# A two-layer graph attention kernel: a layer's last eight superchunks in the step with split sums, in a new order

## The chip, the cores and the metric

The kernel runs on one core of one Trainium2 chip, as one program. The metric is device time in microseconds (us) for one execution: median 4116.05 us of 3 runs of the kernel before (4113.4 to 4126.3).

## What is computed

There are 6250 nodes with 256 features and 200000 edges, sorted by destination. The reference is a pre-norm residual block around two graph attention layers (4 heads, then 1). Cut to what matters:

```python
h = relu(layernorm(x))
# one layer, called twice (heads h=4 f=64, then h=1 f=256):
te = relu(edge_attr @ We + be) * exp(x @ Wo + bo)[src]       # edge features
s2, d2, ea2 = add_self_loops(src, dst, te)                   # loop = mean of a node's edges
hx = (x @ Wg).reshape(n, h, f)
al = leaky_relu((hx*a_s).sum(-1)[src] + (hx*a_d).sum(-1)[dst] + ((ea2@Wge)*a_e).sum(-1), 0.2)
al = exp(al - segment_max(al, dst)[dst])
al = al / segment_sum(al, dst)[dst]
out = segment_sum(hx[src] * al, dst) + b
# layer 0: x = relu(out + x); layer 1: x = out + x; then + h, and + the input
```

## The kernel before, in words

**Tables.** A prologue writes a table T0 with one row per node (projected features, logit parts, norm factors). Layer 0 reads it and writes T1, the same kind of table, which layer 1 reads.

**Superchunks.** The edges are cut into 66 superchunks per layer (`NS`): 64 of 24 chunks of 128 edges, then one of 14 and one of 13. Both layers together make 132 steps k; s = k mod 66 is a step's number in its layer, `st` is its state, `pv` the step before it, `pr` the one before that, `nx` the next. Two edges of the work cross superchunks: a node whose edges are split over two of them is joined by a carried row.

**One superchunk, by engine.**

- GpSimd (POOL) fetches its source rows: `gather` (L881) issues one indirect DMA per chunk into `G`. There are three buffers, taken in turn (k mod 3), so the gather of step k+1 needs the sums of step k-2 to be done. In layer 1 it also needs T1.
- Edge features: `rphase1` (L965 on TensorE, L970 or L968 on ScalarE: two halves, product then relu, into `R`; one PSUM tile `y`, so the second half's product waits for the first half's relu), then `rphase2` (L979) and `adst` (L1038) into the PSUM tile `zad`, then `edge_rows` on VectorE (transpose L1052 or L1050, reduce L1055).
- Logits: `logits` (L1066 to L1081, VectorE; L1066 is the first instruction that needs the gathered rows), `ends` (transpose into `lf`, L1089, TensorE), `links` (L1099, L1101 on VectorE, then the transpose L1106 on TensorE), `maxima` (L1116 to L1143; its L1123 or L1120 needs L1106).
- Values: `scale` (L1174, VectorE, all rows times their weights), `carried` (L1156 to L1164, adds the carried row to chunk 0), `onehots` (L1009, VectorE, the matrix `S`).
- Sums: `sums` (L1185, TensorE): two instructions per chunk, `S` times `G`, into the PSUM tile `u`. `evict` (L1190, ScalarE) copies it to `U`, `carry` (L1196, L1198) forms the carried row.
- Nodes: `finish` (L1209 to L1274 in layer 0, L1214 to L1302 in layer 1; VectorE with three or one ScalarE operations), and in layer 0 `rows1` (L1280, L1282), `rows2` (L385), `rows3` (L389 on VectorE, L1292 on ScalarE, L1321 the write to T1 from SyncE).
- `spread` (L994, L995) once per pair of steps, `parts` (L1019 to L1024), `blocks` (L1031), and in layer 0 a few index instructions per step (`index_on`, L532 to L568).

**Order.** Everything is issued in the program's order, written out by hand; no scheduler moves instructions. Each engine runs its own in that order. There are four kinds of step:

- The plain step (loop body of `edges`): all sums of `pv` between the parts of `nx` and the links of `st`, and `finish` of the step two back.
- The step that enters (s + 1 = `tight`): plain, and then the first half of its own sums, one more `onehots` (for `nx`) and one more `finish` (for `pv`).
- `tight` (s >= `tight`): the first half of the sums of `st` is issued in its own step, right after `scale`; the rest follows in the next step, in two pieces, one before and one after the links' transpose (method `meet`). With `tight = NS - 4` these are s = 62, 63 and 64; s = 61 enters. The one of s = 64 has `final` set: there the nodes of s = 62 and s = 63 are finished and their T1 rows written, because the next layer's first gather (`src1`) needs T1 up to there. The rows of the last two superchunks are added to that gather by products (`added`, L849, L852).
- `last` (s = 65).

Of the kernel before, what the change touches and what calls it, by code (L numbers as in the profile page):

```python
# [32 lines left out]
C = 24  # L33
# [45 lines left out]
class Kernel:  # L79
# [311 lines left out]
    def indices(self, wp):  # L391
# [20 lines left out]
        self.base_f = base = cp.tile([P, NS], F32, name="base")  # L412
        V.tensor_copy(base, scf[:, 0, :])
        last, qbase, qlast = scf[:, 1, :], scf[:, 3:7, :], scf[:, 7:11, :]
        yield

# [41 lines left out]
        yield  # L458
        ll = wp.tile([P, NS], F32, name="ll", bufs=1)
        V.tensor_sub(ll, last, base)  # L460
        self.lsel = cp.tile([P, NS], F32, name="lsel")
        V.tensor_scalar(self.lsel, ll, self.iota_p, None, op0=OP.is_equal)
# [109 lines left out]
    def edges(self, ctx):  # L572
        nc = self.nc
        self.gp += [self.pool(f"gath{i}", 1, ctx) for i in range(1, 3)]
        self.sp = self.pool("onehot", 2, ctx)
        self.lp = self.pool("loads", 2, ctx)
        self.wp = self.pool("work", 2, ctx)
        self.np_ = self.pool("nodes", 2, ctx)
        self.xp = self.pool("index", 1, ctx)
        self.ps_y = self.pool("ps_y", 1, ctx, space=PSUM)  # L580
        self.ps_1 = self.pool("ps_1", 1, ctx, space=PSUM)
        self.ps_f = self.pool("ps_f", 1, ctx, space=PSUM)
        self.lf = self.ps_1.tile([P, 512], F32, name="lf")
        nc.vector.memset(self.lf[0:4, 0:1], -BIG)
        offs = np.concatenate([[0], np.cumsum(self.cs)]).tolist()
        steps = [dict(L=L, s=s, C=self.cs[s], o=offs[s], k=L.l * self.NS + s)
                 for L in self.L for s in range(self.NS)]
        self.state = {0: None, 1: None}
        self.early = self.cs[0] if self.NS > 1 else 0
        self.steps = steps  # L590
        self.nodes(steps[0])
        self.load_lb(0)
        self.load_ea(0)
        self.load_fl(0)
        self.gather(steps[0], self.CX)
        if self.NS % 2:
            self.load_lb(1)
        self.spread(steps[0])
        self.parts(steps[0])
        self.blocks(steps[0])  # L600
        drain(self.rphase1(steps[0]))
        self.load_ea(1)
        self.rphase2(steps[0])
        self.adst(steps[0])
        self.edge_rows(steps[0])

        pv = pf = pr = None

        tight = max(self.NS - 4, 1)
        self.ahead, self.rest = 1, None  # L610
        for k, st in enumerate(steps):
            nx = steps[k + 1] if k + 1 < len(steps) else None
            for q in steps[k + 1:k + 3]:
                if q["L"] is st["L"] and "tw" not in q:
                    self.nodes(q)
            self.load_lb(k + 2)
            left = self.groups[self.ahead][0] - 2 - k if self.ahead < len(self.groups) else 99
            if self.rest is None and left <= 2:
                gi = self.index_load(self.ahead, self.xp)
                self.rest = self.index_group(self.ahead, self.xp, gi)  # L620
            if st["s"] + 1 == self.NS:
                self.last(st, pv, nx)
                pv = pf = pr = None
                continue
            if st["s"] >= tight:
                self.tight(st, pv, pr, nx)
                self.index_on(left)
                pr, pv = pv, st
                continue
            self.gather(nx)  # L630
            drain(self.rphase1(nx))
            self.load_ea(k + 2)
            drain(self.logits(st))
            self.ends(st)
            self.spread(nx)
            self.parts(nx)
            if pv and "u" not in pv:
                self.sums(pv)
            self.links(st)
            self.load_fl(k + 1)  # L640
            self.blocks(nx)
            if k != self.NS:
                self.onehots(st)
            if pf:
                drain(self.finish(pf))
            if pv and "U" not in pv:
                self.evict(pv)
                self.carry(pv)
            if pf:
                self.rows1(pf)  # L650
            self.rphase2(nx)
            self.adst(nx)
            drain(self.maxima(st))
            if pf:
                self.rows2(pf)
            if k == self.NS:
                self.onehots(st)
            drain(self.scale(st))
            self.carried(st)
            enter = st["s"] + 1 == tight  # L660
            if enter:
                self.sums(st, 0, self.pieces(st)[0])
            elif st["s"] == 0:
                self.sums(st)
            if pf:
                self.rows3(pf)
            self.edge_rows(nx)
            if enter:
                self.onehots(nx)
                if pv:  # L670
                    drain(self.finish(pv))
                pr = pv
            elif st["s"] == 0:
                self.evict(st)
                self.carry(st)
            self.index_on(left)
            pf, pv = pv, st
            if k == 0 and self.early:
                self.redirect()
        self.flag()  # L680
# [9 lines left out]
    def pieces(self, st):  # L690

        c = st["C"]
        return (c + 1) // 2, c - c // 3

    def meet(self, st, pv, nx):

        p1, p2 = self.pieces(pv) if pv else (0, 0)
        drain(self.logits(st))
        self.ends(st)
        if nx:  # L700
            self.spread(nx)
            self.parts(nx)
        if pv:
            self.sums(pv, p1, p2)
        self.links(st)
        if pv:
            self.sums(pv, p2)
        self.load_fl(st["k"] + 1)

    def tight(self, st, pv, pr, nx):  # L710


        final = nx["s"] + 1 == self.NS
        self.gather(nx)
        self.meet(st, pv, nx)
        self.blocks(nx)
        if final:
            self.evict(pv)
            self.carry(pv)
            if pr:  # L720
                self.rows1(pr)
                self.rows2(pr)
                self.rows3(pr)
            drain(self.finish(pv))
            drain(self.maxima(st))
            self.rows1(pv)
            self.rows2(pv)
        else:
            drain(self.maxima(st))
            self.evict(pv)  # L730
            self.carry(pv)
            if pr:
                self.rows1(pr)
                self.rows2(pr)
        drain(self.rphase1(nx))
        self.load_ea(st["k"] + 2)
        self.rphase2(nx)
        self.adst(nx)
        if final:
            self.rows3(pv)  # L740
        drain(self.scale(st))
        self.carried(st)
        self.sums(st, 0, self.pieces(st)[0])
        if pr and not final:
            self.rows3(pr)
        self.edge_rows(nx)
        self.onehots(nx)
        if not final:
            drain(self.finish(pv))

    def last(self, st, pv, nx):
# [6 lines left out]
            nc.sync.dma_start(v[:, :early * P], self.srow.partition_broadcast(P))  # L758
        if not pv:
            self.onehots(st)  # L760
        self.meet(st, pv, None)
        if nx:
            nc.vector.tensor_scalar(self.src, self.src, 2.0, None, op0=OP.mult)
        drain(self.maxima(st))
# [687 lines left out]
def drain(g):  # L1452
    for _ in g:
        pass
# [93 lines left out]
```

## Time and profile before

| what | us |
|---|---|
| median of 3 runs | 4116.05 (4113.4 to 4126.3) |
| profiled execution, its own time | 4109.04 |
| span of its trace | 4107.1 |
| POOL busy | 2988.5 (73% of the span), 3158 instructions |
| VectorE (DVE) busy | 2872.1 (70%) |
| TensorE (PE) busy | 2807.1 (68%), granted clock 0.789 of full speed on average |
| ScalarE (ACT) busy | 545.5 (13%) |
| first gather of the stream / last gather's end | 89.62 / 4067.93 |
| layer 0: last gather's end; layer 1: first gather's start | 2058.5; 2097.34 |

The start of a step's `logits` is its first L1066 in the timeline. I call the time from the end of a step's gather to there its lag. At the end of both layers it reads as follows (all from the timelines of POOL and VectorE):

| step | gather | logits start | lag |
|---|---|---|---|
| 57 | 1802.2 to 1831.8 | 1840.6 | 8.8 |
| 58 | 1832.1 to 1862.2 | 1871.1 | 8.9 |
| 61 (enters) | 1923.1 to 1953.3 | 1959.9 | 6.7 |
| 62 | 1953.6 to 1983.5 | 1998.4 | 15.0 |
| 63 | 1983.8 to 2013.6 | 2029.9 | 16.3 |
| 64 (final) | 2013.9 to 2031.5 | 2061.7 | 30.2 |
| 65 (last) | 2042.5 to 2058.5 | 2096.2 | 37.7 |
| 127 (enters) | 3944.1 to 3973.9 | 3976.0 | 2.1 |
| 128 | 3974.2 to 4004.1 | 4009.3 | 5.2 |
| 129 | 4004.4 to 4034.1 | 4036.9 | 2.8 |
| 130 (final) | 4034.4 to 4051.6 | 4058.8 | 7.2 |
| 131 (last) | 4051.9 to 4067.9 | 4079.8 | 11.9 |

In a row of the timeline the columns are start, length (both us), engine, line, operation, tiles and shapes, how many were merged, and in brackets how long the engine had been idle before it and on what.

### The profile page before, as it was taken

What the parts mean: (1) busy time and instruction counts of PE and PEld (TensorE: products, weight loads), DVE (VectorE), ACT (ScalarE), POOL (GpSimd) and SP (SyncE); (2) the same over time, 40 slices, a digit from 0 to 9 for tenths busy, and PEclk for the clock granted to TensorE, in tenths of its full rate; (3) what the DMA queues carried; (4) which work ended last, traced back from release to release, by engine and by line L of the source; (5) the groups of instructions that cost most, each with busy time, mean ns of one, the idle gap of its engine ahead of it and who ended that gap; (6) DMA issues with size and microseconds to landing.
All of it is one profiled execution on the core that took longest, in us unless ns stands there. A gap on an engine that the chain in (4) does not pass through costs nothing.

```text
span 4107.1 us, 34953 instructions
## 1 busy us (share of the span) xinstructions
PE 2807.1 (68%) x10144; PEld 1848.2 (45%) x10144; DVE 2872.1 (70%) x6571; ACT 545.5 (13%) x1256; POOL 2988.5 (73%) x3158
## 2 busy tenths in 40 slices
PE   7677677776777777777676666656666566665766
PEld 5344454444444444445444444434444344443444
DVE  8677777878778787787756666566665666656566
ACT  5111111111111111111111010010100101001001
POOL 2777777777777777777647777777777777777774
PEclk9778787787787887878887777877778777777778
DMA  6555554555555555555435455555445545555543
GB/s 213 157 149 143 155 149 137 154 149 138 151 149 145 146 151 151 139 155 148 122 99 151 131 144 142 136 139 145 134 137 145 142 132 143 142 137 137 145 132 82
DMA packets 246795, 584.74 MB, mean 142 GB/s; under 512 B 63162, under 2 KB 103640, under 8 KB 246530
## 3 DMA queue, kind: packets, MB, share of 16 engines
q0 software_dynamic: 150144, 422.82, 39.4%
q1 hardware_dynamic: 96035, 158.96, 12.3%
q8 instruction: 81, 1.33, 0.1%
q14 instruction: 119, 0.97, 0.1%
q10 hardware_dynamic: 416, 0.67, 0.1%
HBM read 547.98 MB, written 34.34 MB: 142 GB/s over the span
## 4 chain that ended last, share of the span: by engine, by line
POOL 38%; PE 24%; DVE 18%; issue 15%; DMA 2%; ACT 2%; DVEq 0%; SPq 0%; ACTq 0%; POOLq 0%
POOL G L881 38%; PE u L1185 19%; DVE G L1174 8%; PE y L965 2%; DMA G<-T,src 1%; DVE lb L994 1%; PE fin L1196 1%; DVE rt L1052 1%; ACT R L970 1%; PE fin L1280 1%; ACT carry L1198 1%; DVE G L1163 1%; DVE S L1009 0%; DVE t1row L389 0%; DVE G L1143 0%
## 5 line engine op out<-in xcount | busy, mean ns | idle before, releaser
L881 POOL DMA_INDIRECT G<-T,src x3114 | 2970.2, 954 | 1075.2 <-issue 995.8
L1185 PE MATMUL u<-G,S 128*128 128x270 f32 (+1 forms) x6252 | 1700.2, 438 | 26.3 <-DVE G L1174 26.3
L1185 PEld LDWEIGHTS u<-G,S 128*128 128x128 f32 x6252 | 1354.5, 219 | 370.6 <-issue 37.8
L1174 DVE TENSOR_TENSOR G<-G,kps 128x6144 f32<-128x6144 f32 (+2 forms) x140 | 853.2, 6099 | 0.0
L965 PE MATMUL y<-ea,webd 64*128 64x384 f32 (+1 forms) x1056 | 514.1, 617 | 447.1 <-ACT R L970 442.2
L965 PEld LDWEIGHTS y<-ea,webd 64*128 64x128 f32 x1056 | 215.3, 226 | 670.2 <-ACT R L970 523.1
L1009 DVE TENSOR_TENSOR S<-kps,loc 128x3072 f32<-128x3072 f32 x132 | 436.1, 3304 | 0.0
L1089 PE MATMUL lf<-ident,fb 128*36 128x128 f32 (+1 forms) x132 | 53.4, 404 | 531.6 <-DVE fb L1081 307.5
L1089 PEld LDWEIGHTS lf<-ident,fb 128*36 128x36 f32 (+1 forms) x132 | 15.7, 119 | 647.5 <-DVE fb L1081 365.9
L970 ACT ACTIVATE R<-y,webd 128x768 f32<-128x768 f32 x260 | 231.9, 892 | 555.4 <-PE y L965 555.3
L1120 DVE SCALAR_TENSOR_TENSOR m<-fpen,lf,m 128x24 f32<-128x24 bf16 (+1 forms) x66 | 16.6, 252 | 360.2 <-PE lf L1106 359.9
L979 PE MATMUL zad<-R,wea 128*64 128x384 f32 (+1 forms) x1056 | 211.9, 515 | 0.9 <-ACT R L970 0.6
L1066 DVE TENSOR_TENSOR G<-rt,G 128x96 f32<-128x96 f32 (+1 forms) x132 | 30.1, 228 | 255.4 <-DMA G<-T,src 249.8
L1123 DVE TENSOR_TENSOR mt<-fpen,lf 128x96 f32<-128x96 bf16 (+1 forms) x66 | 16.6, 252 | 241.6 <-PE lf L1106 241.6
L1190 ACT ACTIVATE U<-u 128x270 f32<-128x270 f32 (+1 forms) x132 | 51.8, 393 | 798.4 <-PE u L1185 798.4
L1052 DVE STREAM_TRANSPOSE rt<-zad 128x768 f32<-128x768 f32 (+1 forms) x130 | 124.5, 958 | 26.7 <-PE zad L1038 26.7
L1024 PE MATMUL zad<-a,Q 128*128 128x12 bf16 (+1 forms) x132 | 23.5, 178 | 168.8 <-DVE a L1022 168.8
L1223 ACT ACTIVATE mw<-mw,mg 128x2 f32<-128x2 f32 x66 | 19.6, 298 | 863.6 <-DVE mg L1222 863.6
L994 DVE TENSOR_TENSOR lb<-lb,kps 128x1536 bf16<-128x1536 bf16 (+1 forms) x68 | 112.9, 1660 | 11.7 <-DMA lb<-locrow 11.7
L979 PEld LDWEIGHTS zad<-R,wea 128*64 128x64 f32 x1056 | 68.7, 140 | 98.4 <-issue 62.2
L1196 PE MATMUL fin<-U,lsel 128*1 128x270 f32 (+1 forms) x260 | 79.1, 385 | 41.6 <-ACT U L1190 23.2
L1099 DVE TENSOR_TENSOR_SCAN cl<-fl,cl,lf 4x129 f32<-4x129 f32 (+1 forms) x130 | 60.8, 468 | 53.2 <-PE zad L1024 52.4
(213 smaller groups left out, 2260.8 us busy)
## 6 DMA issues: line engine op xcount, KB each, us to landing
G<-T,src POOLq DMA_INDIRECT x3114, 2.8
ea<-in_ea_dram SPq DMA_DIRECT2D x64, 768.0 KB
lb<-locrow SPq DMA_DIRECT2D x64, 384.0 KB
T<-t1row SPq DMA_DIRECT2D x66, 260.0 KB
tw<-T SPq DMA_DIRECT2D x66, 258.0 KB
tw<-T SPq DMA_DIRECT2D x66, 134.0 KB
tw<-in_x_dram SPq DMA_DIRECT2D x66, 128.0 KB
out_dram<-fb SPq DMA_DIRECT2D x64, 128.0 KB
```

What stands on the lines that cost most here:

```text
L881: nc.gpsimd.indirect_dma_start(out=G[:, c, 0:L.TW], out_offset=None, in_=self.rows[L.l][0:n * (1 + L.l), :], in_offset=bass.IndirectOffset ...
L965: nc.tensor.matmul(y[:, o], self.webd[l][r, :], ea[r, w], start=True, stop=True)
L970: nc.scalar.activation(R[:, i, :32 * c].rearrange("p (b n) -> p b n", b=2), y.rearrange("p (b n) -> p b n", b=2)[:, :, :16 * c], AF.Relu, ...
L979: nc.tensor.matmul(st["zad"][i * PH:(i + 1) * PH, o], self.wea[l][0], R[:, i, w], start=True, stop=False)
L994: V.tensor_tensor(lb[:, :, :n], lb[:, :, :n], self.k_part.unsqueeze(2).to_broadcast([P, i, n]), op=OP.is_equal)
L1009: nc.vector.tensor_tensor(st["S"][:, c0:c1, :], self.k_iota.unsqueeze(1).to_broadcast(w), self.loc[:, o + c0:o + c1].unsqueeze(2).to_broad ...
L1052: V.transpose(rv[:, :32 * c].rearrange("p (b n) -> p b n", b=2), z.rearrange("p (b n) -> p b n", b=2)[:, :, :16 * c])
L1089: self.nc.tensor.transpose(self.lf[0:e.shape[1], 1:P + 1], e, self.ident)
L1099: V.tensor_tensor_scan(cl[:H, :], fl[:H, :], lf[:H, 0:P + 1], init, op0=OP.add, op1=OP.max)
L1174: nc.vector.tensor_tensor(v, v, pw[:, c0:c1, :].unsqueeze(3) .to_broadcast([P, c1 - c0, H, L.F]), op=OP.mult)
L1185: nc.tensor.matmul(st["u"][:, :L.W], S[:, i, :], G[:, i, 0:L.W], start=(j == 0), stop=(j == c - 1))
L1196: nc.tensor.matmul(pr[0:1, :L.W], self.lsel[:, s:s + 1], U[:, :L.W], start=True, stop=True)
```

## The change

`tight` becomes `NS - 8`: the steps s = 58 to 64 of each layer run in the method `tight` (before: 62 to 64), and s = 57 enters (before: 61). The method itself gets another order:

- The first product of `nx`'s edge features (half of `rphase1`) is issued ahead of everything, then a small piece of `pv`'s sums (3 of 24 chunks), then the second half, and `load_ea` behind it. Only then come `logits` and `ends` of `st`. Before, `rphase1` and `load_ea` came after the node rows of `pr`, late in the step.
- Between `parts` and `links` stand 3 chunks of `pv`'s sums (before 4), behind `links` the last 6 (before 8).
- `rphase2` and `adst` come ahead of `carry` and the rows of `pr`; `edge_rows` comes ahead of `carried` and of the sums.
- The step ahead of the final one issues all 24 chunks of its own sums at once (`begin`), so the final step has none of `pv`'s left to do. There `finish(pv)` comes ahead of `rows3(pr)`; `rphase1` stays late.
- `last` splits the rest of `pv`'s sums at 8 of 14 chunks instead of 10.

The core of the diff:

```diff
-        tight = max(self.NS - 4, 1)
+        tight = max(self.NS - 8, 1)
...
             if enter:
-                self.sums(st, 0, self.pieces(st)[0])
+                self.begin(st, nx)
...
     def pieces(self, st):
         c = st["C"]
-        return (c + 1) // 2, c - c // 3
+        return (c + 1) // 2, (c + 1) // 2 + c // 8, (c + 1) // 2 + c // 4
+
+    def begin(self, st, nx):
+        self.sums(st, 0, C if nx["s"] + 2 == self.NS else self.pieces(st)[0])
...
     def tight(self, st, pv, pr, nx):
         final = nx["s"] + 1 == self.NS
+        p0, p1, p2 = self.pieces(pv)
         self.gather(nx)
-        self.meet(st, pv, nx)
+        y = self.rphase1(nx)
+        if not final:
+            next(y)
+            self.sums(pv, p0, p1)
+            drain(y)
+            self.load_ea(st["k"] + 2)
+        drain(self.logits(st))
+        self.ends(st)
+        if final:
+            self.evict(pv)
+        self.spread(nx)
+        self.parts(nx)
+        if not final:
+            self.sums(pv, p1, p2)
+        self.links(st)
+        if not final:
+            self.sums(pv, p2)
+        self.load_fl(st["k"] + 1)
         self.blocks(nx)
         if final:
-            self.evict(pv)
             self.carry(pv)
             if pr:
                 self.rows1(pr)
                 self.rows2(pr)
+            drain(self.finish(pv))
+            if pr:
                 self.rows3(pr)
-            drain(self.finish(pv))
             drain(self.maxima(st))
             self.rows1(pv)
             self.rows2(pv)
+            drain(y)
+            self.load_ea(st["k"] + 2)
         else:
             drain(self.maxima(st))
             self.evict(pv)
+        self.rphase2(nx)
+        self.adst(nx)
+        if final:
+            self.rows3(pv)
+        else:
             self.carry(pv)
             if pr:
                 self.rows1(pr)
                 self.rows2(pr)
-        drain(self.rphase1(nx))
-        self.load_ea(st["k"] + 2)
-        self.rphase2(nx)
-        self.adst(nx)
-        if final:
-            self.rows3(pv)
         drain(self.scale(st))
+        self.edge_rows(nx)
         self.carried(st)
-        self.sums(st, 0, self.pieces(st)[0])
-        if pr and not final:
-            self.rows3(pr)
-        self.edge_rows(nx)
+        self.begin(st, nx)
         self.onehots(nx)
         if not final:
+            if pr:
+                self.rows3(pr)
             drain(self.finish(pv))
```

The number and kind of instructions stay as they are, except that some products of the sums and transposes fall into other places of each engine's order.

More of the change, by code (lines that the diff above doesn't have):

```diff
@@ L692, in pieces, with tight @@
         c = st["C"]
-        return (c + 1) // 2, c - c // 3
-    def meet(self, st, pv, nx):
-        p1, p2 = self.pieces(pv) if pv else (0, 0)
+        return (c + 1) // 2, (c + 1) // 2 + c // 8, (c + 1) // 2 + c // 4
+    def begin(self, st, nx):
+        self.sums(st, 0, C if nx["s"] + 2 == self.NS else self.pieces(st)[0])
+    def tight(self, st, pv, pr, nx):
+        final = nx["s"] + 1 == self.NS
+        p0, p1, p2 = self.pieces(pv)
+        self.gather(nx)
+        y = self.rphase1(nx)
[4 more added lines that the diff above has]
+            self.load_ea(st["k"] + 2)
         drain(self.logits(st))
         self.ends(st)
[L700 to L703, printed above, removed]
+        if final:
[3 more added lines that the diff above has]
+        if not final:
             self.sums(pv, p1, p2)
         self.links(st)
-        if pv:
+        if not final:
             self.sums(pv, p2)
         self.load_fl(st["k"] + 1)
-    def tight(self, st, pv, pr, nx):
-        final = nx["s"] + 1 == self.NS
-        self.gather(nx)
-        self.meet(st, pv, nx)
         self.blocks(nx)
         if final:
-            self.evict(pv)
             self.carry(pv)
@@ L760, in last @@
             self.onehots(st)
-        self.meet(st, pv, None)
+        drain(self.logits(st))
+        self.ends(st)
+        if pv:
+            p0, p1, _ = self.pieces(pv)
+            self.sums(pv, p0, p1)
+        self.links(st)
+        if pv:
+            self.sums(pv, p1)
+        self.load_fl(st["k"] + 1)
         if nx:
```

## The prediction

> **What bounds the kernel now.** I read the page's chain of waits first, then the group of its leading line, then POOL's own waits.
>
> ```profile
> POOL G L881 38%; PE u L1185 19%; DVE G L1174 8%; PE y L965 2%; DMA G<-T,src 1%; DVE lb L994 1%; PE fin L1196 1%; DVE rt L1052 1%; ACT R L970 1%; PE fin L1280 1%; ACT carry L1198 1%; DVE G L1163 1%; DVE S L1009 0%; DVE t1row L389 0%; DVE G L1143 0%
> L881 POOL DMA_INDIRECT G<-T,src x3114 | 2970.2, 954 | 1075.2 <-issue 995.8
> ```
>
> The gather leads the chain. One costs 0.954 us busy and about 0.30 of issue; in POOL's timeline they stand 1.25 us apart, so 24 chunks take 30.1 us and 3114 take about 3893 of the 4107.1 us. Nothing done on other engines shortens that. What is left are the places where POOL stands still. Its waits, by what released them:
>
> ```profile
> POOL G L881 <- DVE al L1072: 38.8, 1, 38.8
> POOL out_dram L1330 <- DVE oidx L1329: 23.7, 1, 23.7
> POOL G L881 <- PE u L1185: 11.1, 1, 11.1
> POOL G L881 <- DVE G L852: 7.2, 1, 7.2
> ```
>
> One wait each: 11.1 us in layer 0 ahead of step 65's gather (from 2031.5, until step 62's sums free the buffer), 38.8 ahead of layer 1's first gather (until 2097.34), 7.2 behind that, 23.7 at the end. In between the stream runs. So the change counts only in what it does to the last lags of each layer.
>
> The 38.8 are booked to a VectorE instruction that has nothing to do with T1. The SyncE row for step 63's rows is at 2091.82, behind a load of 768 KB issued at 2090.85; the DMA view has the transfers busy until 2096.3, and the gather starts at 2097.34. I take the landing of those rows as the true releaser: `rows3` of step 63 in the final step sets layer 1's start.
>
> Next, what a split step costs. Step 62 and the final step 64 on VectorE:
>
> ```profile
> 1998.43 0.26 DVE L1066 TENSOR_TENSOR G<-rt,G 128x96 f32<-128x96 f32 x1
> ...
> 2005.35 0.25 DVE L1123 TENSOR_TENSOR mt<-fpen,lf 128x96 f32<-128x96 bf16 x1 [3.14 <-PE lf L1106]
> ...
> 2019.79 0.98 DVE L1052 STREAM_TRANSPOSE rt<-zad 128x768 f32<-128x768 f32 x1 [4.35 <-PE zad L1038]
> ...
> 2029.87 0.26 DVE L1066 TENSOR_TENSOR G<-rt,G 128x96 f32<-128x96 f32 x1 [0.20 <-issue]
> ...
> 2061.70 0.22 DVE L1066 TENSOR_TENSOR G<-rt,G 128x56 f32<-128x56 f32 x1 [0.20 <-DMA G<-T,src]
> ...
> 2077.05 0.43 DVE L389 TENSOR_TENSOR t1row<-fin,bias 128x260 f32<-128x260 f32 x1 [11.40 <-PE fin L385]
> ```
>
> Step 62 takes 31.44 us, longer than the gather's 30.1, of which 3.14 wait for the links' transpose (behind 4 chunks of sums) and 4.35 for late edge features. Without both it is 23.95, or 23.4 without 0.58 of index work. The final step stops 11.40 us for the rows of step 62, which stand on TensorE behind the second half of step 63's sums.
>
> **The edge features ahead.** No operation is added. TensorE now has `y`, 3 chunks, `y` ahead of the logits, and `rphase2` and `adst` right behind the sums, under `scale` (6.5 us, one instruction). Together they need 1.5 + 0.5 us (rows of L979 and L1038), so `zad` is there before `scale` ends: the 4.35 go. Cover gone, they would come back. `load_ea` on SyncE is only issued earlier, and what follows it there (T1 writes) with it; it still has half a step to land. Gathers run on POOL past all this.
>
> New waits: the second `y` waits for ScalarE's relu of the first, which stands in ScalarE's order behind `finish` of the step before; its last ScalarE row (1996.76, 0.42 long) ends 0.4 us ahead of `finish`'s end, and only index work lies between that and the logits. So TensorE comes to a stop there, with the second `y`, `ends`, `parts`, 3 chunks and the links' transpose queued behind. Relu (0.90) ends at about logits + 0.5, less index work; `y` then takes 1.55 us in most rows.
>
> **The smaller piece, and the clock.** The wait of 3.14 is the price of 4 chunks at a slow clock:
>
> ```profile
> 2001.11 3.95 PE L1185 MATMUL u<-G,S 128*128 128x270 f32 x8
> 2005.24 3.91 PE L1185 MATMUL u<-G,S 128*128 128x270 f32 x16
> ```
>
> That is 0.99 us per chunk after 5.5 idle us, then 0.49. The Trainium skill (TensorE: Matmul & The Clock Gate, Part 1) says why: the array falls to half clock after an idle window of about 3.4 us and needs about as long of steady work to get back. That speaks against this change, which cuts the sums finer and puts a stop ahead of the second `y`. From the end of `scale` TensorE has 5.6 (12 chunks) + 1.55 + 1.4 us, VectorE about 11.5 until the logits, so the stop is 3 to 4 us: by the rule `y` runs cold, and one row shows that price (2.93 us). Then `lf` is there at 3.8, where VectorE wants it at 2.5 (1.3 lost), and the 3 chunks are half warm (0.9 more): about 2.2 us of VectorE waiting, less where `spread` or index work lies ahead. By the trace's common rows (1.55 and 0.49) it is 0.6. All cold it is 3.3, none at all 0. I take 1.3 per step, between the two.
>
> **Entering.** The step that enters did cost 38.5 (61) against 29.3 to 30.5 around it; one-hots 3.26 plus nodes 4.85 are 8.1. Moved to step 57: logits of 58 at 1840.6 + 30.5 + 8.1 = 1879.2, lag 17 against 8.9. The buffer rule holds: step 60's gather (1892.7) needs step 57's sums, done at about 1888.
>
> **Layer 0, split steps.** Each is 23.4 + 1.3 + index (0.6, 0.0, 1.5, 0.9, 0.6 for 58 to 62) + 2.0 for `spread` in 59 and 61. Logits at: 1904.5 (59), 1931.2, 1957.4, then 1985.5 (62) and 2015.6 (63), where the gather's end plus 2.0 us of landing holds them. Against 1998.4 and 2029.9. Step 63 was 31.83, less 3.13 and 4.01, plus 1.3: 26.0. Logits of 64 at 2041.6, before 2061.70: 20.1 earlier. Step 62's sums are done at about 2026, before 2031.5, so the wait of 11.1 goes; by itself that gives nothing, as the logits are later than the gather. With 3.3 us of wait per step I get 2048.3 (13.4 earlier), with none 2040.3 (21.4).
>
> **Layer 0, final step.** From logits 64 to layer 1's first gather took 35.64. Step 63's 24 chunks now start at the end of its `scale`, 11.4 us ahead of logits 64, and take 11 to 12.6: `U` is there within about a microsecond and `finish(63)` starts at +3.96, right behind `blocks`, where the 11.40 began. Rows of 62 pass on TensorE meanwhile. All behind moves 11.4 up; the rows of 63 lose about 0.4, since the PSUM tile is freed by `rows3(62)` later, and gain up to 2 if warm. I take 11.6 (9 to 13). Layer 0 together 31.7. The last step's rows keep their 6 to 7 us of slack to the end of that first gather, so the 7.2 stay.
>
> **Layer 1's end.** The lag stays at its floor of 2 until step 129: logits 4036.1 (before 4036.9). Step 129 loses the wait for `zad` (0.93) and one chunk of 0.9: logits 130 at 4056.1 against 4058.8. There `finish(129)` waited 5.41 for `U`; now all 24 chunks start at `scale`'s end, 6.4 us ahead of logits 130, and hold back `ends`, so `links` waits about 3.3 instead. `edge_rows` then waits about 1.3. Logits 131 about 4 earlier than 4079.85; the rest is unchanged. 4.2 (0 to 8).
>
> Sum: 31.7 + 4.2 = 36, rounded. Against the profiled execution's 4109.04 that is 4073; it lies 7 below the median of the runs, and I predict the median: 4116.05 - 36 = 4080.
>
> **Rivals.**
>
> *Part of the waits stays.* The stop ahead of the second `y` costs 3 us or more in every step, or the final step is held elsewhere. Layer 0 gives 13.4 + 5 to 9, layer 1 nothing: 18 to 22, so 4094 to 4098. For it: cold rows are common here. Against it: 2 us more of VectorE work (`spread`) hide it in every other step.
>
> *The lag is not what counts.* If SyncE's load ahead of step 63's rows, or another gather condition, set layer 1's start, only layer 1's 4 us and some of the final step come: 4104 to 4113, no change. Against it: the last transfer ends 1.0 us ahead of the gather, and the load waits for `y` of 65, which moves along.
>
> *Slower.* The waits move and do not vanish. Seven long steps stand where three did, entered with a lag of 17. Without a floor, logits 64 come at 2028.5 + 6w for w us of waiting per step; with 11.6 back in the final step it is even at w = 7.5, as much as step 62's 3.14 + 4.35. The place is the first `y`'s relu behind `finish`, with TensorE's whole order behind it. At w = 10 it is 15 us: 4131. Against it: the relu needs only `finish`'s ScalarE rows, which end ahead of the logits, so nothing behind it can hold more than a cold `y` and cold chunks, about 3.3.
>
> **How the numbers follow.** Forecast 0.80 (4066 to 4093), part stays 0.10, no change 0.06, slower 0.04. A measurement of this kernel can tell 0.3%, 12.3 us, from no change. Faster by more: 0.80 + 0.10 = 0.90; within 0.06; slower 0.04. Range: the low end is 21.4 + 13 + 8 = 42 below the median and another 7 for the profile's distance to it, rounded; the high end takes in the first rival: 4066 to 4098.
>
> **What would show it.** Right: POOL's 11.1 wait is gone, L1123's wait in steps 58 to 63 is near 1 and L1052's none, the logits of 63 start 2 us behind their gather, the 38.8 shrink to about 18 (from 2047.8 to 2065.6), and L389's 11.40 is gone. Wrong: a lag that does not fall from step 58 on, a POOL gap before step 63, or a first gather of layer 1 later than 2075.

## The result, and the profile after

| | before | after |
|---|---|---|
| median of 5 runs, us | 4121.02 (4113.4 to 4126.3) | 4088.22 (4082.09 to 4094.02) |
| profiled execution, us | 4109.04 | 4088.22 |
| span of its trace, us | 4107.1 | 4086.3 |

The ratio of after to before is 0.9922 (95% interval 0.9905 to 0.9939): faster by 32 us of the 4116.05 (25 to 39), where the forecast had 36. All of after's runs lie in its range. Two more runs of before raised its median from 4116.05 to 4121.02, which is 5 of the 8 us between the 4080 forecast and the 4088 measured. Kernels close to after, run later on chips where before takes the same time, fit this; on two other chips, where before takes 18 to 20% longer, the sign was another, as the experiments show.

Line numbers in after stand 16 higher from L881 on (L881 is L897, L1066 is L1082, L1123 is L1139, L1185 is L1201). The page of after gives for the chain of waits and the gather:

```profile
POOL G L897 37%; PE u L1201 19%; DVE G L1190 9%; PE y L981 2%; DMA G<-T,src 2%; DVE lb L1010 1%; DVE rt L1068 1%; PE fin L1212 1%; ACT R L986 1%; PE fin L1296 1%; DVE G L1179 1%; DVE S L1025 1%; ACT carry L1214 1%; DVE G L1159 0%; DVE t1row L389 0%
L897 POOL DMA_INDIRECT G<-T,src x3114 | 2969.9, 954 | 1057.7 <-issue 989.5
```

The same 3114 gathers, 954 ns each, lead the chain as before. What changed is in the waits view of POOL:

```profile
POOL G L897 <- PE u L1201: 20.5, 1, 20.5
POOL G L897 <- PE lf L1122: 20.3, 19, 6.2
POOL out_dram L1346 <- DVE oidx L1345: 20.1, 1, 20.1
POOL G L897 <- DMA T<-t1row: 7.2, 1, 7.2
```

The wait of 11.1 us is gone. The 38.8 ahead of layer 1's first gather have become 20.5 (booked to yet another instruction; rows_first_2 below shows what released it). The 23.7 at the end are 20.1, the 7.2 stay. New are the 20.3 in 19 pieces: before had 6.4 in 9 from the same line. They lie in the plain steps (6.2 of them at 195 us), where no instruction differs.

The timeline of VectorE in after, steps 62, 63 and the final 64, answers to the rows shown of before:

```profile
1998.91 0.26 DVE L1082 TENSOR_TENSOR G<-rt,G 128x96 f32<-128x96 f32 x1 [0.20 <-DMA G<-T,src]
...
2004.94 0.26 DVE L1139 TENSOR_TENSOR mt<-fpen,lf 128x96 f32<-128x96 bf16 x1 [2.07 <-PE lf L1122]
...
2013.71 0.98 DVE L1068 STREAM_TRANSPOSE rt<-zad 128x768 f32<-128x768 f32 x1
...
2025.43 0.26 DVE L1082 TENSOR_TENSOR G<-rt,G 128x96 f32<-128x96 f32 x1 [0.39 <-DMA G<-T,src]
...
2032.21 0.26 DVE L1139 TENSOR_TENSOR mt<-fpen,lf 128x96 f32<-128x96 bf16 x1 [2.21 <-PE lf L1122]
...
2052.64 0.22 DVE L1082 TENSOR_TENSOR G<-rt,G 128x56 f32<-128x56 f32 x1 [0.21 <-DMA G<-T,src]
...
2059.49 0.17 DVE L1253 TENSOR_TENSOR mg<-U,mw 128x4 f32<-128x4 f32 x1 [1.58 <-ACT mw L1251]
...
2067.35 0.43 DVE L389 TENSOR_TENSOR t1row<-fin,bias 128x260 f32<-128x260 f32 x1 [2.21 <-PE fin L385]
```

The wait of the transpose of `zad` (4.35 before) is gone, the one for the links' transpose has only fallen from 3.14 to 2.07 and 2.21, step 63 waits 0.39 for its gather, and the final step no longer stops 11.40 us for the rows of step 62. Its second L389, the rows of step 63, waits 2.21 us as it did before.

The profiled executions differ by 20.8 us, 12 less than the medians. Cut into segments, with the same cuts for every kernel (us, from the timelines of POOL and VectorE):

| profiled run | start of step 57's gather | from there to layer 1's first gather | of it, logits of 64 to that gather | step 123's gather to the end | span |
|---|---|---|---|---|---|
| before | 1802.2 | 295.2 | 35.6 | 283.5 | 4107.1 |
| after | 1811.4 | 266.8 | 25.6 | 280.5 | 4086.3 |
| range_only | 1804.9 | 311.5 | 35.4 | 283.4 | 4125.1 |
| order_only | 1819.1 | 279.7 | 25.4 | 280.8 | 4105.6 |
| late_y | 1816.9 | 308.3 | 25.6 | 283.0 | 4134.6 |
| half_begin | 1805.6 | 274.7 | 32.1 | 283.1 | 4090.8 |
| rows_first_2 | 1816.6 | 261.9 | 18.2 | 282.1 | 4092.9 |
| both_2 | 1803.4 | 257.2 | 17.5 | 277.1 | 4070.9 |

The first column is the plain part, which has the same instructions in all eight; it ends anywhere between 1802 and 1819 us. I take this for chance from one execution to the next: five runs of after alone lie 12 us apart. It is as large as some of the effects sought. So I read effects from the segments, and ratios from the repeated runs.

The layer 0 segment is not free of this chance either, since the lag at step 57 differs: 8.8 us in before, 9.3 in after, but 4.3 in range_only, 11.3 in order_only and 11.7 in late_y. Where a later step catches up with its gather and starts at the floor (a lag of about 2 us, in which the last rows land), the difference is lost; where none does, it stays in the segment. Counted from the logits of step 57 to layer 1's first gather, before takes 256.7, after 227.2, range_only 277.2, order_only 238.3 and late_y 266.6.

After: 28.4 us in layer 0 (295.2 to 266.8), 3.0 at layer 1's end, 0.6 at layer 1's start (step 66's gather to step 67's, 40.0 to 39.4), less 9.3 for the later start and 2.0 in layer 1's plain steps: 20.7.

### The profile page after: what moved, and what is told of

It is laid out like the page before. It is cut to its first block, busy times and chain, and to the rows that moved or that the text cites. A ratio compares the mean times of both kernels' runs of the same rounds, so it can differ in the third digit from the quotient of the medians.

```text
span 4086.3 us, 34956 instructions
## 1 busy us (share of the span) xinstructions
PE 2823.3 (69%) x10144; PEld 1852.9 (45%) x10144; DVE 2873.2 (70%) x6571; ACT 546.0 (13%) x1256; POOL 2988.1 (73%) x3158
## 4 chain that ended last, share of the span: by engine, by line
POOL 37%; PE 24%; DVE 20%; issue 14%; DMA 3%; ACT 2%; DVEq 0%; SPq 0%; ACTq 0%; POOLq 0%
POOL G L897 37%; PE u L1201 19%; DVE G L1190 9%; PE y L981 2%; DMA G<-T,src 2%; DVE lb L1010 1%; DVE rt L1068 1%; PE fin L1212 1%; ACT R L986 1%; PE fin L1296 1%; DVE G L1179 1%; DVE S L1025 1%; ACT carry L1214 1%; DVE G L1159 0%; DVE t1row L389 0%
## 5 line engine op out<-in xcount | busy, mean ns | idle before, releaser
L897 POOL DMA_INDIRECT G<-T,src x3114 | 2969.9, 954 | 1057.7 <-issue 989.5
L1201 PE MATMUL u<-G,S 128*128 128x270 f32 (+1 forms) x6252 | 1718.8, 441 | 44.2 <-DVE G L1190 44.2
L1201 PEld LDWEIGHTS u<-G,S 128*128 128x128 f32 x6252 | 1359.7, 221 | 403.5 <-DVE G L1190 51.7
L1190 DVE TENSOR_TENSOR G<-G,kps 128x6144 f32<-128x6144 f32 (+2 forms) x140 | 853.3, 6100 | 0.0
L1082 DVE TENSOR_TENSOR G<-rt,G 128x96 f32<-128x96 f32 (+1 forms) x132 | 30.2, 229 | 272.9 <-DMA G<-T,src 266.6
L1139 DVE TENSOR_TENSOR mt<-fpen,lf 128x96 f32<-128x96 bf16 (+1 forms) x66 | 16.7, 253 | 237.0 <-PE lf L1122 237.0
L1068 DVE STREAM_TRANSPOSE rt<-zad 128x768 f32<-128x768 f32 (+1 forms) x130 | 124.6, 958 | 11.7 <-PE zad L1054 11.7
```

The source lines that it names most:

```text
L897: nc.gpsimd.indirect_dma_start(out=G[:, c, 0:L.TW], out_offset=None, in_=self.rows[L.l][0:n * (1 + L.l), :], in_offset=bass.IndirectOffset ...
L1068: V.transpose(rv[:, :32 * c].rearrange("p (b n) -> p b n", b=2), z.rearrange("p (b n) -> p b n", b=2)[:, :, :16 * c])
L1190: nc.vector.tensor_tensor(v, v, pw[:, c0:c1, :].unsqueeze(3) .to_broadcast([P, c1 - c0, H, L.F]), op=OP.mult)
L1201: nc.tensor.matmul(st["u"][:, :L.W], S[:, i, :], G[:, i, 0:L.W], start=(j == 0), stop=(j == c - 1))
```

## The experiments

My theory: the gather stream is the bound up to the end of each layer, where the lag counts. The lag falls because (a) edge features issued among the sums are ready early, and (b) the final step has no sums left. Rivals: the order does nothing and the number of split steps does it all (or the reverse), and the landing of step 63's T1 rows isn't what layer 1 waits for. Each kernel is compared with runs of before on the same chip.

**range_only**, before with one constant changed:

```diff
-        tight = max(self.NS - 4, 1)
+        tight = max(self.NS - 8, 1)
```

> The kernel before with the one line of the range changed (the last eight superchunks in the old split step). My theory: the gain is in the shorter step. The old split step has 23.4 us of VectorE work, 0 to 1.5 of index work, 2.0 of spread in every other one, and 7.5 of waits, more than the gather's 30.1; entered four steps earlier, the lag grows from 17 at step 58 to about 28 at step 63, and the logits of step 64 start about 11 us later than in the kernel before. The final step is as before. So 8 to 14 us slower than before. Rival (the early start of a superchunk's sums is what helps, whatever the order): 5 to 10 us faster than before.

Measured 4143.97 (before there 4125.26), ratio 1.0056 (1.0036 to 1.0076), about 23 us slower; the layer 0 segment is 16.3 longer, or 20.4 counted from the logits of step 57. The direction is as expected, the size twice as large. The reason is the edge features: each of steps 58 to 63 waits 2.7 to 3.1 for the links and 3.9 to 8.3 for `zad`, 8.6 together in the mean, so a step takes 31.7 to 37.4 us and the lag grows from 14.2 (58) to 36.4 (64). The TensorE timeline of step 59 and the windows view of two of its rows say why it can be 8.3:

```profile
1929.65 2.93 PE L965 MATMUL y<-ea,webd 64*128 64x384 f32 x4
1933.62 2.92 PE L965 MATMUL y<-ea,webd 64*128 64x384 f32 x4 [1.05 <-ACT R L970]
1936.48 3.13 PE L979 MATMUL zad<-R,wea 128*64 128x384 f32 x8
```

```profile
core 0: us, PE busy (x) PEld busy (x) DVE busy (x) ACT busy (x) POOL busy (x), PEclk, DMA share, GB/s
1929.70:1932.50 2.80, 2.80 (x5) 1.11 (x4) 2.02 (x6) 0.00 (x0) 2.19 (x3) 0.50 0.40 104
1933.70:1936.40 2.70, 2.70 (x4) 1.08 (x4) 0.00 (x0) 0.00 (x0) 2.09 (x3) 0.50 0.48 119
```

PEclk is the granted clock as a share of full speed. Behind the small products of the node rows, which all wait for ScalarE, TensorE is at 0.50, and `y`, `y`, L979 take 8.98 us where the same rows at full clock take 1.55, 1.55 and 1.51. More split steps in the old order are a loss.

**order_only**, after with `NS - 4` put back:

```diff
-        tight = max(self.NS - 8, 1)
+        tight = max(self.NS - 4, 1)
```

> The kernel after with the split step for the last four superchunks only, as before the change. My theory: entered at step 61 with a lag of 15 at step 62, steps 62 and 63 take about 26.5 and 27.2 instead of 31.4 and 31.8, the final step to layer 1's first gather about 25.6 instead of 35.6: 19 to 20 us in layer 0, 2 to 3 at layer 1's end, 20 to 23 us faster than before, about 10 slower than the kernel after. L1139's waits are near 2.1, L1068 does not wait. Rival (the range carries most of it): at most 10 faster than before.

Measured 4103.12, ratio 0.9943 (0.9919 to 0.9967), some 23 us faster, as expected. The layer 0 segment is 15.5 shorter than before's. Together with range_only this makes a square: order alone -15.5, range alone +16.3, both -28.4 (from the logits of step 57: -18.4, +20.4, -29.5). The four extra split steps bring 11 to 13 us in the new order and cost 16 to 20 in the old one. Neither part does it all.

**late_y**, after with the edge features back behind the node rows in all split steps:

```diff
         y = self.rphase1(nx)
         if not final:
-            next(y)
             self.sums(pv, p0, p1)
-            drain(y)
-            self.load_ea(st["k"] + 2)
...
             self.evict(pv)
-        self.rphase2(nx)
-        self.adst(nx)
...
                 self.rows2(pr)
+            drain(y)
+            self.load_ea(st["k"] + 2)
+        self.rphase2(nx)
+        self.adst(nx)
```

> The kernel after with the edge features (both halves of rphase1, load_ea, rphase2, adst) behind the node rows in the steps that are not final, where they stood before; the sums' pieces and all else as after. My theory: the transpose L1068 waits about 3.3 us again in each of steps 58 to 63 of layer 0 (4.35 before, less one for two chunks fewer ahead of it), the lag does not reach its floor, and logits of step 64 start 18 to 22 us later than in the kernel after; in layer 1 the slack takes most of it. So 10 to 15 us faster than before instead of about 32. Rival (the features' place is free, since scale hides them anyway): within 4 us of the kernel after.

Measured 4130.00, ratio 1.0016 (1.0001 to 1.0030): 5 to 7 us slower than before, only just clear of no difference, where I had expected it 10 to 15 faster. The VectorE timeline of step 60:

```profile
1972.24 0.25 DVE L1137 TENSOR_TENSOR mt<-fpen,lf 128x96 f32<-128x96 bf16 x1 [2.04 <-PE lf L1120]
...
1988.26 0.98 DVE L1066 STREAM_TRANSPOSE rt<-zad 128x768 f32<-128x768 f32 x1 [7.25 <-PE zad L1052]
```

The wait for `zad` comes back, as it should, but with 5.7 to 7.2 us in steps 58 to 62 instead of the 3.3 I gave it, and 3.6 in step 63. With the links' 2.2 the steps lose 8.4 us each, the layer 0 segment is 41.5 longer than after's (39.3 from the logits of step 57), and the lag at step 64 is 36.2 (after: 11.5). The mechanism held and the size was wrong, for two reasons that the timelines show. In step 58 all products run at full clock, with the same lengths as in before's step 62, and the wait is 5.74 for 4.35: in the new order `edge_rows` stands ahead of `carried` and the T1 row, so the 1.40 us of VectorE work that covered the wait before (2014.04 to 2015.44) come behind it. In step 60 the second `y` takes 2.30 for 1.55, and L993, the product for `zad`, 3.88, where step 58 has it done in 2.56; the granted clock fell to 0.50 during that `y`, and the wait is 7.25. Late features cost about as much in the new order as in the old (6.2 us per step in the mean, 5.6 in range_only), and of the parts taken away one at a time their place is the dearest.

**half_begin**, after without the rule that the step ahead of the final one issues all 24 chunks:

```diff
     def begin(self, st, nx):
-        self.sums(st, 0, C if nx["s"] + 2 == self.NS else self.pieces(st)[0])
+        self.sums(st, 0, self.pieces(st)[0])
...
         if final:
-            self.evict(pv)
...
-        if not final:
-            self.sums(pv, p1, p2)
+        self.sums(pv, p0 if final else p1, p2)
         self.links(st)
-        if not final:
-            self.sums(pv, p2)
+        self.sums(pv, p2)
...
         if final:
+            self.evict(pv)
             self.carry(pv)
```

> The kernel after, but the step ahead of the final one issues only half of its own sums, and the final step does the other half in two pieces around the links, as before the change; finish(pv) stays ahead of rows3(pr). My theory: in the final step of layer 0 the nodes of step 63 wait 7 to 8 us for U (evict behind 12 chunks), layer 1's first gather comes 6 to 8 us later than in the kernel after; in layer 1 the wait of 4.0 at L1115 turns into 5 to 6 at L1230: together 7 to 9 us slower than the kernel after, 22 to 26 faster than before. Rival (the swap of finish and rows3 alone took the 11.40 away): within 3 us of the kernel after.

Measured 4101.96, ratio 0.9950 (0.9934 to 0.9966), some 11 us of the gain gone. From the logits of 64 to layer 1's first gather 32.1 instead of 25.6, and one row of VectorE's timeline holds it:

```profile
2059.41 0.15 DVE L1222 TENSOR_SCALAR cnt<-U 128x1 f32<-128x1 f32 x1 [7.20 <-ACT U L1203]
```

`finish(63)` waits for the sums that are left. At layer 1's end it waits 5.42 for the same (after: 4.04 at the links instead), and that end is 2.6 longer. 6.5 + 2.6 = 9.1, at the end of the 7 to 9 expected; by the ratio it is some 21 faster than before, for 22 to 26. The rival, that the swap of `finish` and `rows3` does it alone, fails.

**Another chip.** The next four ran on another chip, where before takes 4929.82 (4921.02 to 4938.96): after unchanged (after_again), the T1 rows of step 63 written earlier (rows_first), no sums between `parts` and `links` (no_piece), and `NS - 6` (eight_to_six):

```diff
             self.rows2(pv)
+            self.rows3(pv)
             drain(y)
...
-        if final:
-            self.rows3(pv)
-        else:
+        if not final:
```

is rows_first, and

```diff
-        if not final:
-            self.sums(pv, p1, p2)
         self.links(st)
         if not final:
-            self.sums(pv, p2)
+            self.sums(pv, p1)
```

is no_piece.

> The kernel after, unchanged, as the measure for the three beside it. 30 to 36 us faster than before. In its trace the stretch from the start of step 57's gather to layer 1's first gather is 264 to 270 us (295.2 in the kernel before), whatever the plain steps ahead of it took.

> The kernel after, but in the final step rows3(pv), the T1 rows of step 63, comes right behind rows2(pv), ahead of both halves of rphase1 and of the next layer's edge load. My theory: the landing of these rows releases layer 1's first gather. The write is issued 4 to 5 us earlier and does not stand behind 768 KB, so the first gather comes 6 to 7 us earlier against logits of step 64 (18.5 to 19.5 instead of 25.6); then the rows of step 65, which had about 1 us of slack in the kernel after, hold the second gather, so 3 to 4 us of it remain. Rival (the buffer or another wait of the gather holds it, as the profile's name for the releaser, a product of the sums, says): no change of the 25.6.

> The kernel after, with no sums between parts and links: the 3 chunks are issued with the last 6, behind the links' transpose. My theory: the wait of 2.1 at L1139 in the split steps is these 3 chunks at half clock, so it falls below 0.5; the sums still end under scale. Steps 58 to 63 are 2 us shorter each, but the gather holds step 63's logits already, so only that step's 2 us and the little wait ahead of it count in layer 0, and 2 in layer 1: 3 to 5 us faster than the kernel after. Rival (the piece is free, or the sums behind it get late and hold edge_rows and the carried row): no gain, or L1068 waits 1 to 3 us.

> The kernel after with the split step for the last six superchunks. My theory: the lag of 17 to 19 after entering falls by 3 per step; entered at step 59 it has five steps instead of six to fall, two fewer than needed to reach the floor of 2, so the logits of step 64 start 5 to 9 us later and the kernel is 4 to 9 us slower than the kernel after, 23 to 30 faster than before. Rival (any four or more do the same): within 3 us of the kernel after.

| | median, us | ratio |
|---|---|---|
| after_again | 4959.34 | 1.0053 (1.0038 to 1.0069) |
| rows_first | 4955.72 | 1.0048 (1.0035 to 1.0061) |
| no_piece | 4975.20 | 1.0091 (1.0078 to 1.0104) |
| eight_to_six | 4938.27 | 1.0023 (1.0011 to 1.0036) |

Every expected time was missed, and after itself is slower than before there. rows_first is within the noise of after_again. no_piece is slower by a further 16 us: its wait at the links' transpose is gone, as expected, but ahead of the links (L1113) it waits 11.1 and 15.3 us in steps 59 and 60, where after_again waits 0.7 and 5.6. Why stays open. The trace of after_again: a gather still takes 952 ns and L1190 6100 ns in the mean, as in the profile of after above. But short VectorE instructions that follow each other without a wait there stand apart here, as in the node work of a plain step,

```profile
1122.01 0.25 DVE L1231 TENSOR_SCALAR mw<-U,cnt 128x4 f32<-128x4 f32 x1 [0.94 <-DVE mg L1230]
1123.44 0.16 DVE L1233 TENSOR_TENSOR mg<-mg,tw 128x4 f32<-128x4 f32 x1 [1.18 <-DVE mw L1231]
1126.24 0.16 DVE L1235 SCALAR_TENSOR_TENSOR mw<-mg 128x4 f32<-128x4 f32 x1 [2.64 <-remote]
```

and POOL waits for the sums all along the layers, by its waits view:

```profile
POOL G L897 <- PE lf L1122: 672.8, 111, 13.7
POOL G L897 <- PE u L1201: 216.1, 14, 44.2
```

(20.3 in 19 waits and one of 20.5 in the profile of after above). So in this trace the chain of VectorE and TensorE bounds most steps, not the gather. That would make a split step cost more than it brings, and fits the ratios (with fewer split steps the loss is smaller), but there is no trace of before on this chip, so the cause of the turned sign is argued and not shown. What holds on both chips is the final step, where rows_first brings 18.2 us from the logits of 64 to layer 1's first gather, after_again 25.6.

**no_piece_2 and both** (no_piece and rows_first together) ran on a third chip, with before at 4870.98 (4864.92 to 4879.12):

> The same kernel as no_piece, for a chip on which the kernel before takes about 4120 us (told by the gathers, 1.25 us apart without other waits). My theory as there: L1139's wait of 2.1 falls below 0.5 in the split steps, L1068 does not wait, 3 to 5 us faster than the kernel after, which was 0.9922 of before: 0.990 to 0.992. The stretch from step 57's gather to layer 1's first gather 261 to 265 us against 266.8. Rival (the sums, later now, hold the end of scale): L1068 waits 1 to 3 us and nothing is gained.

> no_piece and rows_first in one kernel: no sums between parts and links, and in the final step the T1 rows of step 63 ahead of the edge features. My theory: from logits of step 64 to layer 1's first gather 18 to 19 us instead of 25.6; the second gather, held by the rows of step 65, gains 3 to 4 of these 7; with 3 to 5 of no_piece 6 to 9 us faster than the kernel after: 0.988 to 0.991 of before. Rival (layer 1's second gather is held by the last rows alone): only no_piece's gain, 0.990 to 0.992.

Measured 4915.97, ratio 1.0095 (1.0080 to 1.0109), and 4919.56, ratio 1.0099 (1.0083 to 1.0115): both 1% slower than before. They say nothing of kernels on a chip where the gather is the bound, and with no run of after beside them they only fit what no_piece gave.

**rows_first_2 and both_2**, rows_first and both again, on a chip where before takes 4124.02 (4113.92 to 4134.77):

> The same kernel as rows_first, for such a chip, so that what the piece between parts and links is worth can be read from the two. My theory: 18.2 to 19 us instead of 25.6, 3 to 4 us faster than the kernel after: 0.990 to 0.992 of before, its waits at L1139 near 2.1 as in the kernel after, 3 to 5 us slower than both_2. Rival: no faster than the kernel after.

> The same kernel as both, once more for a chip on which the kernel before takes about 4120 us. My theory as there: 18 to 19 us from logits of step 64 to layer 1's first gather instead of 25.6, 6 to 9 us faster than the kernel after: 0.988 to 0.991 of before. Rival (the second gather is held by the last rows, and the piece is free): 0.991 to 0.993, as the kernel after.

rows_first_2: 4083.50, ratio 0.9897 (0.9881 to 0.9912). The interval overlaps after's, so the times alone do not show it faster than after; the trace shows where it gains. From the logits of 64 to layer 1's first gather 18.2, after 25.6. POOL's waits now name the releaser:

```profile
POOL G L896 <- DMA T<-t1row: 28.0, 2, 16.6
```

Writing step 63's rows earlier, and nothing else, starts layer 1 7.4 us sooner: it is their landing that the first gather waits for. The packets of the traces agree: in before, after, rows_first_2 and both_2 the last transfer ends 1.2 us ahead of that gather. In after, the timelines of SyncE and POOL show why it lands late:

```profile
2071.63 0.40 SPq L922 DMA_DIRECT2D ea<-in_ea_dram  x1
2072.61 0.33 SPq L1337 DMA_DIRECT2D T<-t1row  x1
2078.21 0.94 POOL L897 DMA_INDIRECT G<-T,src  x1 [20.46 <-PE u L1201]
```

The rows are ready in VectorE at 2067.78, but their norm (L1308) stands on ScalarE behind two relus, so that the write is issued at 2072.61, 1.0 behind a load of 768 KB, and the gather starts 5.6 later. In rows_first_2 the write goes out first:

```profile
2075.60 0.33 SPq L1336 DMA_DIRECT2D T<-t1row  x1
2078.42 0.95 POOL L896 DMA_INDIRECT G<-T,src  x1 [16.64 <-DMA T<-t1row]
```

Counted from the start of L389, the write is issued after 0.7 us instead of 5.3, and the gather starts 2.8 behind it instead of 5.6. So 4.6 of the 7.4 come from the earlier issue and 2.8 from the faster landing; that the load ahead of it made the landing slow fits, but no run moved the load alone. Only about half of the 7.4 stays: from step 66's gather to step 67's are now 43.2 us (after 39.4), since the rows of the last step don't move with it, and POOL's wait for them is 11.4 instead of 7.2.

both_2: 4076.71 (4071.32 to 4079.13), ratio 0.9882 (0.9866 to 0.9898). Its interval lies below after's, so by the ratios this version beats both kernels where before takes some 4120 us; after itself did not run on this chip, and on the third chip the same kernel was 1% slower than before. No step of 58 to 63 waits for the links any more; steps 62 and 63 start their logits at the floor,

```profile
1990.48 0.26 DVE L1079 TENSOR_TENSOR G<-rt,G 128x96 f32<-128x96 f32 x1 [4.03 <-DMA G<-T,src]
...
2018.31 0.26 DVE L1079 TENSOR_TENSOR G<-rt,G 128x96 f32<-128x96 f32 x1 [3.71 <-DMA G<-T,src]
```

with 4.03 and 3.71 us to spare, so the stream takes back what the links gave in the steps before. Against rows_first_2 the layer 0 segment is 4.7 shorter and layer 1's end 5.0, but the intervals of the two ratios overlap, so what the piece between `parts` and `links` costs is not settled by the times.

## Why the prediction was right, step by step

**The bound, and the wait of 38.8.** Right, on the chips where before takes some 4120 us. There the stream holds until the last steps, and the wait belonged to the T1 rows of step 63, not to the VectorE line that the view booked: rows_first_2 moved it by moving that write. The rival "the lag is not what counts" allowed some 4 us and part of the final step; the layer 0 segment fell by 28.4. Its doubt about the load ahead of step 63's rows was sound all the same: what stands ahead of that write costs 7.4 us.

**Entering.** Step 57 took 40.0 us, my 30.5 + 8.1 = 38.6, and the lag at 58 was 18.9 for 17. It cost nothing in this execution, because step 63 started at the floor. That was close: the forecast had the logits of 62 and 63 both held by their gathers, with 4.8 us to spare at 63 by its own figures; measured, those of 62 started 5.8 us behind their gather, and those of 63 waited 0.39 for theirs. In rows_first_2, which has the same steps 57 to 63 and was entered with a lag of 20.2 at 58, step 63 started 5.2 behind its gather and missed the floor by 3 us. So that the earlier errors dropped out was in part luck.

**The edge features ahead.** Right: no wait for `zad` in steps 58 to 63. What it costs when the cover is gone I had read from one row, 4.35; late_y and range_only show 3.6 to 8.3 per step.

**The stop at the second `y`, and the clock.** Here a term was mis-sized. The wait per step, W, was 0.48, 2.17, 1.88, 2.21, 2.07, 2.21 us in steps 58 to 63, 1.84 in the mean, where I took 1.3. TensorE's timeline in step 62, and its clock in the two halves of it:

```profile
1999.71 1.55 PE L981 MATMUL y<-ea,webd 64*128 64x384 f32 x4 [3.56 <-ACT R L986]
2001.19 0.34 PE L1105 MATMUL lf<-ident,fb 128*36 128x128 f32 x1
2001.62 0.17 PE L1040 MATMUL zad<-a,Q 128*128 128x12 bf16 x1
2001.64 3.05 PE L1201 MATMUL u<-G,S 128*128 128x270 f32 x6
2004.62 0.28 PE L1122 MATMUL lf<-ident,cl 36*128 36x36 f32 x1
```

```profile
1999.80:2001.20 1.40, 1.40 (x5) 0.58 (x6) 1.26 (x7) 0.00 (x0) 0.99 (x2) 1.00 0.61 189
2001.70:2004.60 2.90, 2.90 (x7) 1.77 (x6) 1.13 (x4) 0.50 (x1) 2.28 (x3) 0.50 0.83 252
```

In the second view the columns are the stretch, its length, the busy time and instructions of PE, PEld, DVE, ACT and POOL, the granted clock, the DMA share and GB/s. The stop was 3.56 us, within the 3 to 4 worked out. But `y` right behind it ran at full clock (1.00, 1.55 us), and only then did the clock fall: the 3 chunks ran at 0.50, 1.02 us each, and VectorE waited 2.07. The Trainium skill (TensorE: Matmul & The Clock Gate, Part 1) speaks of a free-running window; that fits a fall that comes after the work has begun again, which these rows show. I had the cold row at the wrong instruction; its sum by the rule, 2.2, was nearer than my middle value. Because step 63 started at the floor (lag 2.0), five of the six waits were taken back, and the error counts once: step 63 took 27.2 us for 26.0. The rival "part of the waits stays" was right that they stay, and asked 3 us or more per step for them; they came to 1.84.

**The final step.** 25.6 us for 24.0. `finish(63)` starts 3.87 behind the logits (3.96 expected) and 11.40 is gone. But its L1253 now waits 1.58 us, before 0.28: ScalarE's L1251, which it needs, stands behind the copy of step 62's rows (L1298, 2058.98). That wait I had not listed. The gain "up to 2 if warm" did not come: L385 takes 2.10 and `y` 1.75 in the final step, as before. half_begin shows the share of the 24 early chunks, 6.5 us here.

**Layer 0 together.** 28.4 for 31.7: 1.8 of the difference lies in steps 57 to 63, 1.6 in the final step.

**Layer 1's end.** 3.0 for 4.2. `links` waits 4.04 there (3.3 expected), `edge_rows` 1.16 (1.3), the lag at 131 is 8.5 for 11.9: 3.4 earlier, 4 expected.

**What was to show it.** POOL's 11.1, L1068's wait and the 11.40 are gone, and the logits of 63 stand 2.0 behind their gather: as forecast. L1139's wait is 2, not 1, and POOL's wait ahead of layer 1 is 20.5, not 18. The first gather of layer 1 came at 2078.2, past the mark of 2075 that I had set for "wrong"; the plain part had ended 9.3 us later in this execution, and counted from step 57 the gather is 28.4 earlier. A mark in absolute time was a poor one.

**The rival "slower"** named a real stop (TensorE waits 3.56 us for the relu behind `finish`), but it costs VectorE 1.84 us per step, far from the 7.5 at which it had the gain used up. Steps that long do turn the sign when the waits come from late features: late_y and range_only lose 8.4 and 8.6 us per step, and both end on the slower side.

## What to carry to other kernels

When one engine streams at a fixed pace, look only at how late its last items are used: a step that is shorter than the stream's lets earlier losses vanish at the floor, a longer one adds up with every repetition, so the number of such steps and their length are to be judged together (here the same four extra steps take off 11 to 13 us in one order and add 16 to 20 in the other). Check too how much is to spare at the floor: here it was 0.39 us. Ahead of a hand-over between stages, find the transfer that really releases the next one and issue it before loads and work that aren't needed yet. And judge a change of under 1% from segments of the trace that the change touches, on more than one chip, with the state in which each segment begins.

## What the runs showed of the hardware that was not expected

Chips differed. The kernel before takes 4121, 4125 and 4124 us in three groups of runs, and 4930 and 4871 on two other chips, each run at one time only. On the chip of after_again the gather and L1190 take the same time each, the mean granted clock of TensorE is 0.728 instead of 0.786, and waits of 0.9 to 2.6 us that the profile puts down to the instruction just before or to nothing it shows stand between short VectorE instructions. After is 0.8% faster than before in the first runs and 0.5% slower on that chip. What makes the difference was not tried and stays open.

The TensorE clock can fall late: after 3.56 idle us it stayed at 1.00 for the first 1.5 us of the work that followed, and then fell to 0.50.
